# Two-layer graph network on one core: the prologue in blocks of four, its weights on two queues beside the table, the sums zeroed block by block

## The chip, the cores and the metric

The kernel runs on one core of a Trainium2 chip. The metric is the device time of one execution in microseconds (us); lower is better. The timed figure is the median of three runs. Beside it stands one more execution that the hardware profiler recorded; every duration of a single instruction below is from that one.

## The reference, cut to what matters

A graph has 6250 nodes with 160 features (64 scalars and 32 three-vectors) and 200000 edges, sorted by their destination. Two message-passing layers run one after the other. Each one mixes the node features linearly, makes a weight vector per edge from the edge's attributes, multiplies the features of the edge's source node by it, and adds the products up over the edges of each destination node.

```python
# layer 0, per node and per edge (layer 1 has the same shape)
x1 = (xs * attr_a) @ Ws_l1_a + (xs * attr_c) @ Ws_l1_c   # and the same for the vectors
weight = silu(edge_attr_10 @ W_fc1) @ W_fc2
edge_feat = weight * x1[edge_src] * edge_attr            # several products
agg = segment_sum(edge_feat, edge_dst, num_segments=n)
out = C_S * self_part + C_X * ((agg @ W_l2_a) + (agg @ W_l2_c)) @ W_l3
# then residual and layer norm; layer 1 follows on the result
```

## The kernel before, in words

**Edges in tiles, tiles in groups.** The edges come in NT = 1563 tiles of 128. Consecutive tiles form 284 groups of 3 to 12 tiles; because the edges are sorted, all edges of a group fall into a window of W = 32 destination nodes. The sums of all nodes stay in SBUF for a whole layer, in two tiles `sm` (128 x 4 x 6304) and `sr` (128 x 6304) (lines 115 and 116).

**The loop.** `windows(i, loads, work)` (from line 465) is run for layer i = 0 and then i = 1. It goes through 391 units of four tiles. Per unit GpSimd (POOL) issues four indirect DMAs, which gather the source nodes' rows of a table in DRAM (line 583); TensorE (PE) makes the hidden layer (`pa`) and the edge weights (`pw`), VectorE (DVE) builds the selection matrices (`sel`, line 617) and the products (`mid`, lines 599 and 604), TensorE adds the products up in PSUM (`pg`), turns the result (`pt`), and VectorE adds it to `sm` and `sr` at a row that it reads from `base` (lines 667 and 669). Gathers run four units ahead of the sums: there are eight gather buffers of two tiles. Node blocks whose sums are complete are finished in between (`second_nodes`, `last_nodes`). At line 404 and 405 `second_nodes` clears the block's sums with VectorE for layer 1.

**The prologue.** All that stands ahead of the loop is straight-line code:

* SP loads the nodes in 7 chunks of 7 blocks (line 124); ACT's queue loads `nv`, the first layer's weights `wl1` by way of `spread` (lines 138 to 155), 15 short runs of `base` (line 171) and the destinations `raw` (line 175).
* From `base` and `raw` it makes `off`, each edge's row within its window (lines 183 to 196), and writes it to DRAM as `rel`; the loop reads it back in pieces, `dr` (line 500). From `off` it works out a flag (lines 199 to 216): whether every edge lies within its window. If not, a general and slow path runs in place of `windows`.
* `first_nodes` (lines 251 to 266) makes the gather table of layer 0. For each of the 49 node blocks it transposes the features with TensorE (two transposes, `turned`, lines 219 to 228), copies both out with ACT, multiplies them by `wl1` (two products: 128 x 256 and 32 x 64, `mixed`, line 230), and combines the two halves with ACT and VectorE. One DMA on SP's queue per chunk writes the rows.
* The weights of the loop are put together in `fc1`, `fc2`, `wsc`, `wh`, `wo`, `rm0`, `rr0`, `rm1`, `rr1` (lines 273 to 351), by DMAs on SP's queue. `rm0` and `rr0` are filled by ten DMAs from SBUF to SBUF out of four products of TensorE (lines 314 to 329).
* GpSimd zeroes `sm` and `sr` whole, in two instructions (line 354).
* The pools of the prologue are given back at line 355 (`prologue.close()`); the loop's `loads` and `edges` pools take that memory.

**What sets the order.** The framework orders the instructions of each engine by a simulation of its own, as far as data allow. In the loop, TensorE's instructions are kept in program order (`pinned`, lines 238 to 248); in the prologue they are not. [...]

## Time and profile before

| | |
|---|---|
| median of three timed runs | 6722.72 us (6715.26 to 6724.2) |
| the profiled execution's own time | 4272.91 us |
| its span | 4271.1 us |
| mean granted TensorE clock in it | 0.908 |
| TensorE busy | 3661.5 us (86% of the span) |
| GpSimd busy | 3021.2 us (71%) |
| VectorE busy | 2957.8 us (69%) |
| first gather starts | 153.58 us |

The profiled execution is 2450 us shorter than the timed median. Busy times count matmuls whose ends are modelled. A line of the groups says: line of the kernel, engine, operation, output<-inputs, shapes, count, then busy time and mean ns of one, then the idle time of that engine just before and what ended most of it.

### The profile page before, as it was taken

How to read it: one execution, taken by the hardware profiler on the slowest of the kernel's cores; microseconds unless marked ns; L12 is line 12 of the kernel's file. 1: busy time of each engine (PE TensorE's matmuls, PEld its weight loads, DVE VectorE, ACT ScalarE, POOL GpSimd, SP SyncE). 2: the span in 40 equal slices, each digit the busy share in tenths (PEclk: the TensorE clock that was granted, in tenths of full speed). 3: DMA queues.
4: the chain of work that ended last, by engine and by line, in shares of the span. 5: the costliest groups of instructions: out<-in, count | busy, mean ns of one | idle time of the engine just before them, and what ended most of it. 6: DMA issues, size and time to landing. Idle time of an engine off the chain costs nothing.

```text
span 4271.1 us, 137680 instructions
## 1 busy us (share of the span) xinstructions
PE 3661.5 (86%) x53873; PEld 2656.1 (62%) x53873; DVE 2957.8 (69%) x10736; ACT 1065.0 (25%) x2506; POOL 3021.2 (71%) x3192
## 2 busy tenths in 40 slices
PE   7787879888999999999988888888888888888887
PEld 4555556566666666666655666666666666666665
DVE  5466666666667677766655777777777777777887
ACT  2211111222222233333221001121222222333443
POOL 2477777777777777766635777777777777777775
PEclk9989999899999999999986988888898898898888
DMA  2233333333333333332212333333443344434443
GB/s 82 67 74 74 77 76 77 80 79 82 79 84 83 83 85 85 81 76 75 71 48 76 93 100 99 99 99 99 102 103 102 97 110 104 106 101 108 107 108 76
DMA packets 312505, 374.13 MB, mean 88 GB/s; under 512 B 98379, under 2 KB 256783, under 8 KB 311851
## 3 DMA queue, kind: packets, MB, share of 16 engines
q0 software_dynamic: 150016, 256.20, 24.4%
q1 hardware_dynamic: 132406, 91.31, 8.0%
q10 hardware_dynamic: 29429, 17.75, 1.4%
q8 instruction: 430, 7.05, 0.7%
q14 instruction: 224, 1.84, 0.1%
HBM read 343.19 MB, written 21.60 MB: 85 GB/s over the span
## 4 chain that ended last, share of the span: by engine, by line
PE 40%; issue 17%; DMA 14%; POOL 13%; DVE 10%; ACT 2%; DVEq 1%; SPq 0%; POOLq 0%; ACTq 0%
POOL g L583 13%; DMA g<-table,src 13%; PE pw L241 12%; PE pg L241 9%; PE pa L241 8%; PE pn L241 7%; DVE mid L604 3%; PE pt L246 2%; DVE sel L617 2%; DVE mid L599 2%; DMA e<-in_e 1%; PE pn L246 1%; DVE sm L667 1%; ACT L363 1%; DVEq L664 1%
## 5 line engine op out<-in xcount | busy, mean ns | idle before, releaser
L583 POOL DMA_INDIRECT g<-table,src x3126 | 2990.1, 957 | 1218.5 <-issue 720.4
L241 PE MATMUL pw<-fc,h 100*128 100x192 f32 (+1 forms) x6252 | 1279.6, 375 | 197.2 <-DVE mid L604 171.3
L241 PEld LDWEIGHTS pg<-mid,sel 128*32 128x32 f32 x40638 | 953.2, 118 | 489.0 <-issue 485.9
L241 PEld LDWEIGHTS pw<-fc,h 100*128 100x128 f32 (+1 forms) x6252 | 955.1, 201 | 352.7 <-issue 162.8
L604 DVE TENSOR_TENSOR mid<-g,pw 128x192 f32<-128x192 f32 x3910 | 1170.2, 346 | 0.0
L599 DVE TENSOR_TENSOR mid<-pw,g 128x256 f32<-128x256 f32 x1564 | 660.8, 423 | 720.2 <-DMA g<-table,src 406.0
L241 PE MATMUL pg<-mid,sel 128*32 128x64 f32 (+4 forms) x40638 | 1130.6, 255 | 0.0
L617 DVE SCALAR_TENSOR_TENSOR sel<-iota,dr,ea 128x128 f32<-128x128 f32 x3126 | 951.4, 346 | 240.4 <-PE pg L241 227.6
L241 PE MATMUL pa<-e,fc 128*100 128x512 f32 (+1 forms) x1566 | 748.8, 563 | 123.1 <-DMA e<-in_e 122.8
L542 ACT ACTIVATE h<-pa 100x512 f32<-100x512 f32 x391 | 233.5, 597 | 1203.0 <-PE pa L241 1176.4
L241 PEld LDWEIGHTS pa<-e,fc 128*100 128x100 f32 (+1 forms) x1566 | 265.5, 193 | 250.9 <-issue 125.3
L554 ACT ACTIVATE h<-pa 128x256 f32<-128x256 f32 x392 | 150.4, 384 | 1022.8 <-PE pa L241 1003.7
L246 PE MATMUL pt<-ident,r 128*96 128x128 f32 (+1 forms) x852 | 229.0, 292 | 15.6 <-DVE sr L669 13.8
L646 ACT ACTIVATE r<-pg 128x96 f32<-128x96 f32 (+1 forms) x568 | 154.9, 274 | 315.4 <-PE pg L241 209.8
L667 DVE TENSOR_TENSOR sm<-pt,sm 96x128 f32 (+1 forms) x568 | 162.7, 286 | 89.6 <-PE pt L246 81.8
L246 PEld LDWEIGHTS pt<-ident,r 128*96 128x96 f32 (+1 forms) x852 | 106.0, 124 | 133.7 <-issue 67.3
L241 PE MATMUL pn<-rm,sm 96*128 96x128 f32 (+4 forms) x980 | 160.4, 318 | 17.2 <-DVE sm L667 14.2
L241 PEld LDWEIGHTS pn<-rm,sm 96*128 96x128 f32 (+3 forms) x980 | 154.3, 218 | 25.2 <-DVE sm L667 18.4
L554 ACT ACT_TABLE_LOAD x94 | 120.6, 1283 | 122.7 <-PE pa L241 99.4
L241 PE MATMUL pn<-rr,sr 64*128 64x128 f32 (+2 forms) x196 | 62.1, 403 | 80.2 <-DVE sr L669 79.2
L241 PE MATMUL pt<-ident,r 128*32 128x32 f32 x2272 | 85.9, 203 | 47.9 <-DVE sr L669 46.2
L241 PEld LDWEIGHTS pt<-ident,r 128*32 128x32 f32 x2272 | 89.5, 118 | 53.7 <-issue 47.5
(118 smaller groups left out, 1508.6 us busy)
## 6 DMA issues: line engine op xcount, KB each, us to landing
g<-table,src POOLq DMA_INDIRECT x3126
e<-in_e SPq DMA_DIRECT2D x781, 64.0 KB
e<-in_e SPq DMA_DIRECT2D x390, 20.0 KB
ea<-in_ea_main SPq DMA_DIRECT2D x64, 96.0 KB
xself<-no ACTq DMA_DIRECT2D x48, 96.0 KB
no<-xself SPq DMA_DIRECT2D x48, 96.0 KB
nx<-in_x_main SPq DMA_DIRECT2D x48, 80.0 KB
xmid<-nx ACTq DMA_DIRECT2D x48, 80.0 KB
```

What stands on the lines that cost most here:

```text
L241: r = nc.tensor.matmul(*args, **kw)
L246: r = nc.tensor.transpose(*args)
L363: nc.scalar.activation(mv[:n, 1:2], mv[:n, 1:2], AF.Sqrt, bias=eps[:n])
L542: nc.scalar.activation(h[:100, :n], p[:100, :n], AF.Silu)
L554: nc.scalar.activation(h[:kk, c0:c1], p[:kk, c0:c1], AF.Silu, scale=0.125)
L583: nc.gpsimd.indirect_dma_start(out=g[:n, j, :], out_offset=None, in_=table[i][:, :], in_offset=bass.IndirectOffsetOnAxis(ap=of(t)[0], axis=0))
L599: nc.vector.tensor_tensor(two, q[:n, :m, 0:2 * S].rearrange("p j (k d) -> p j k d", k=2), gs, OP.mult)
L604: nc.vector.tensor_tensor(o[:, :, at:at + 96].rearrange("p j (c d) -> p j c d", c=3), gv, q[:n, :m, None, w0:w0 + V].to_broadcast([n, m, 3 ...
L617: made["last"] = nc.vector.scalar_tensor_tensor(s[:n, j], iota[:n, None, :].to_broadcast([n, 4, W]), w, e[:, :, None].to_broadcast([n, 4, ...
L646: nc.scalar.activation(r[:, :w], pg[:, :w], AF.Copy)
L664: b = nc.vector.value_load(base[0:1, g:g + 1], min_val=0, max_val=NP - W)
L667: nc.vector.tensor_tensor(sm[:h, :, at], pt[:h, :P].rearrange("p (c w) -> p c w", c=4), sm[:h, :, at], OP.add)
```

## The change

The number of blocks per chunk, `BG`, goes from 7 to 4, and `ZERO = 8` is new. `pinned` is true from the start, so the prologue's TensorE instructions keep the written order, too. The rest, part by part:

```diff
-BG = 7
+BG = 4
+ZERO = 8
+def zeroed(g):
+    b = ZERO + 4 + (GROUPS[g][0] + GROUPS[g][1] - 1) // 4
+    return NP if b >= NB else b * P
...
-    rel = dram.tile([P, NT], F32, name="rel")
...
+    def zero(b):
+        c = slice(b * P, b * P + P if b < NB - 1 else NP)
+        nc.vector.memset(sm[:, :, c], 0.0)
+        nc.vector.memset(sr[:, c], 0.0)
+    pinned = [True]
...
+    first = (const.tile([P, CH, 1], I32, name="src0"), const.tile([P, CH, 4], F32, name="ea0"))
+    nc.sync.dma_start(first[0], a["src_main"][:, :CH, :])
+    nc.sync.dma_start(first[1], a["ea_main"][:, :CH, :])
...
+    spread(l1[:, 0], "Ws_l1_a", "Wv_l1_a", S, nc.scalar)
+    spread(l1[:, 1], "Ws_l1_c", "Wv_l1_c", S, nc.scalar)
     ident = const.tile([P, P], F32, name="ident")
     make_identity(nc, ident)
+    for j, (k, q) in enumerate((("a", nc.scalar), ("c", nc.gpsimd))):
+        for r in range(0, P, V):
+            q.dma_start(l1z[r:r + V, j, :], a[f"Wv_l1_{k}"])
+    nc.gpsimd.dma_start(nv[:, :NB - 1, :], a["nv_main"])
+    nc.gpsimd.dma_start(nv[:tail_n, NB - 1, :], a["nv_tail"])
...
-        while g1 < NG and GROUPS[g1][1] == GROUPS[g0][1] and (g1 + 1 - g0) * GROUPS[g0][1] <= 180:
+        while g1 < NG and GROUPS[g1][1] == GROUPS[g0][1]:
...
-        nc.scalar.dma_start(base[:, g0:g1], bass.AP(tensor=d.tensor, offset=d.offset + t0 * P,
+        nc.gpsimd.dma_start(base[:, g0:g1], bass.AP(tensor=d.tensor, offset=d.offset + t0 * P,
...
-    nc.scalar.dma_start(raw[:, :NT - 1], a["dst_main"][:, :, 0])
-    nc.scalar.dma_start(raw[:tail_e, NT - 1:], a["dst_tail"])
+    nc.gpsimd.dma_start(raw[:, :NT - 1], a["dst_main"][:, :, 0])
+    nc.gpsimd.dma_start(raw[:tail_e, NT - 1:], a["dst_tail"])
...
+    nc.gpsimd.dma_start(fc1[0][:10], a["W_fc1"])
...
+        nc.gpsimd.dma_start(fc2[0][:, at:at + n], a["W_fc2"][:, c0:c0 + n])
...
+        nc.gpsimd.dma_start(w23[:, at:at + n], a[k])
...
+    def turn_nodes(bs, x):
+        m, n = len(bs), rows_of(bs[0])
+        p = psum.tile([P, 512], F32, name="pw", bufs=3)
+        for j in range(m):
+            transpose(p[:, j * P:j * P + n], x[:n, j, 0:P], ident[:n, :n])
+        last = work.tile([P, BG * V], F32, name="xz")
+        nc.vector.tensor_copy(last[:n, :m * V].rearrange("p (j d) -> p j d", d=V), x[:n, 0:m, P:D])
+        z = psum.tile([P, 512], F32, name="pa", bufs=1)
+        transpose(z[:m * V, :n], last[:n, :m * V], ident[:n, :n])
+        xt = work.tile([P, BG * P], F32, name="xt", bufs=2)
+        zt = work.tile([P, P], F32, name="zt", bufs=2)
+        w = (m - 1) * P + n
+        nc.vector.tensor_copy(xt[:, :w], p[:, :w])
+        nc.scalar.activation(zt[:m * V, :n], z[:m * V, :n], AF.Copy)
+        return xt, zt
+    def send_nodes(bs, xt, zt):
...
+        for j, b in enumerate(bs):
+            tag, k = (("pg", 2), ("pn", 1), ("pg", 2), ("pt", 1))[j]
...
+            matmul(q[:, :, 0:P], xt[:, j * P:j * P + n], l1, start=True, stop=True)
+            matmul(q[:, :, P:D], zt[v, :n], l1z[v], start=True, stop=True,
+                   tile_position=(j * V, 0))
+            t = rows[:n, j, :]
+            nc.scalar.activation(t, q[:, 0, :], AF.Copy, scale=nv[:n, b, 0:1])
+            nc.vector.scalar_tensor_tensor(t, q[:, 1, :], nv[:n, b, 1:2], t,
+                                           op0=OP.mult, op1=OP.add)
...
-    off = pre.tile([P, NT], F32, name="off")
+    off = const.tile([P, NT], F32, name="off")
...
+    def check():
...
+        p = psum.tile([P, 512], F32, name="pa", bufs=1)
+        matmul(p[:, :NG], ones, basef, start=True, stop=True)
+        for g0, g1 in segments:
...
+            nc.vector.tensor_tensor(o, o, p[:, g0:g1, None].to_broadcast([P, m, n]), OP.subtract)
...
+        nc.vector.tensor_reduce(ends[:, 0:1], off, AX.X, OP.max)
+        nc.vector.tensor_reduce(ends[:, 1:2], off, AX.X, OP.min)
...
+        transpose(p[:1, :P], over, ident)
...
+    for c, (bs, x) in enumerate(zip(chunks, xs)):
+        now = bs, turn_nodes(bs, x)
+        if previous:
+            send_nodes(previous[0], *previous[1])
+        previous = now
+        if c == 8:
+            check()
+    send_nodes(previous[0], *previous[1])
...
+    for b in range(ZERO):
+        zero(b)
...
-    for t in (sm, sr):
-        nc.gpsimd.memset(t, 0.0)
     prologue.close()
...
+            if c == 0:
+                s, e = first
...
-            nc.sync.dma_start(w[:, :t1 - t0], rel[:, t0:t1])
...
+            return s[:n, k, :], off[:n, t:t + 1], e[:n, k, :]
...
+            if i == 0 and ZERO + 4 + u < NB:
+                zero(ZERO + 4 + u)
```

In words, for the parts that are cut: the flag also asks that a group's window lies in rows that are zeroed by then (`zeroed`). The second layer's weights `wh` and `wo` become one tile `who`, loaded like `wsc` on SP's queue. `rm0` and `rr0` are filled by six copies of VectorE out of PSUM, from eight small products of TensorE, in place of four products and ten DMAs. `rm1` and `rr1` are still loaded by 16 DMAs of SP, and scaled by seven VectorE instructions in place of 16. In the written order the weights of `wsc`, `who`, `fc1[1]`, `fc2[1]`, `rm1` and `rr1` (40 DMAs on SP's queue) stand behind the table's last store. GpSimd's queue issues 29 direct DMAs: 4 of `l1z`, 2 of `nv`, 11 of `base`, 2 of `raw`, 1 of `fc1`, 3 of `fc2`, 6 of `w23`. The loop is otherwise as it was.

## Prediction

> **What bounds the kernel now.** I read the page first. Its largest row is the gather on GpSimd:

> ```profile
> L583 POOL DMA_INDIRECT g<-table,src x3126 | 2990.1, 957 | 1218.5 <-issue 720.4
> ```

> A gather takes 957 ns, and about 300 ns pass to the next one: 3126 x 1.257 = 3929 us of a span of 4271.1. In the profiled execution the loop thus follows GpSimd, and what stands ahead of the first gather is paid in full. It starts at 153.58 us; the change is almost all in that stretch. So next the stretch by stages (columns: window, its length, then busy us of PE, its weight loads, DVE, ACT, POOL; granted clock, DMA share, GB/s):

> ```profile
> 0.00:33.00 33.00, 2.52 (x11) 1.90 (x11) 29.54 (x14) 2.03 (x5) 31.14 (x66) 1.00 0.53 159
> 33.00:60.00 27.00, 26.96 (x88) 17.88 (x87) 12.38 (x37) 6.42 (x27) 0.00 (x0) 1.00 0.17 56
> 60.00:119.80 59.80, 59.80 (x167) 36.39 (x166) 14.20 (x50) 19.60 (x84) 0.00 (x0) 1.00 0.15 43
> 119.80:145.00 25.20, 24.11 (x71) 14.94 (x70) 5.05 (x16) 7.75 (x32) 0.00 (x0) 1.00 0.14 45
> 145.00:154.30 9.30, 0.04 (x1) 0.07 (x1) 2.14 (x6) 0.00 (x0) 0.72 (x1) 1.00 0.19 41
> ```

> Three parts: 33 us with TensorE nearly idle, 111 us in which it is busy throughout, and a tail of 9 us in which it is idle again. The instructions in order of time (start, us, instruction) say why the first part is empty:

> ```profile
> 4.31 27.48 DVE L298 TENSOR_SCALAR own<-nv 128x96 f32<-128x96 f32 x1 [2.45 <-DMA nv<-in_nv_main]
> ...
> 5.33 21.11 POOL L354 MEMSET sm<- 128x25216 f32 x1
> ...
> 26.39 5.34 POOL L354 MEMSET sr<- 128x6304 f32 x1
> ...
> 32.95 1.22 PE L241 MATMUL pt<-wl,xt 128*128 128x256 f32 x2
> ```

> A small VectorE instruction issued at 4.31 ends at 31.79; GpSimd's memsets end at 31.73. VectorE stood still while GpSimd zeroed, and everything waited behind it. In the second part the work on two node blocks repeats every 4.28 us:

> ```profile
> 124.09 1.11 PE L246 MATMUL pw<-ident,xg 128*128 128x128 f32 x4
> ...
> 125.00 1.06 PE L241 MATMUL pt<-wl,xt 128*128 128x256 f32 x2
> ...
> 125.99 0.69 PE L241 MATMUL pt<-wl1z,xt 32*128 32x64 f32 x2
> ...
> 126.60 1.22 PE L241 MATMUL pn<-wl,xt 128*128 128x256 f32 x2
> ...
> 128.37 1.11 PE L246 MATMUL pw<-ident,xg 128*128 128x128 f32 x4
> ```

> From start to start: four transposes 0.91 us (0.23 each), the wide product 0.99, the narrow one 0.61. The third part, from the chain that ended last (start, us, what):

> ```profile
> 144.46 0.30 SPq L266
> ...
> 148.74 1.85 DMA rm<-w23s
> ...
> 152.03 1.56 DMA e<-in_e
> 153.59 1.10 POOL g L583
> ```

> The table's last store goes out at 144.46; then SP issues the last seven of the ten copies into `rm0` and `rr0`, and only when the last has landed (150.59) is the prologue's memory free for the loop's loads.

> **How this stands to the median.** Span 4271.1 plus 1.8 outside is the profiled 4272.9. The median is 6722.7; no view shows the other 2450. There is one hint. The 512-column product `pa`, between 160 and 168 us and then between 190 and 210 us:

> ```profile
> L241 PE MATMUL pa<-e,fc 128*100 128x512 f32 x4 | 3.8, 1059 | 0.0
> L241 PE MATMUL pa<-e,fc 128*100 128x512 f32 x8 | 4.1, 592 | 0.0
> ```

> TensorE runs at about half rate up to 168 us, although the granted clock is printed as 1.00 there. If timed runs stayed at that rate, TensorE would bind: its 3661 us busy times 1.63 (192-column products, 540 to 332 ns) to 1.79 (`pa`) is 5970 to 6550, an estimate, not far below 6723. In that reading, or if gathers are slower there, the prologue is as in the profile (TensorE is at half rate in it already), so I carry the microseconds over unscaled.

> **The change, part by part.**

> *Zeroing.* Off GpSimd go 26.4 us of memset. On VectorE, block by block: the existing clear of one block takes 485 + 165 ns (lines 404, 405), so 8 blocks in the prologue cost 5.2 us beside 100 us of TensorE work, and 42 in the loop 0.65 us per unit of 5.0 us, in which VectorE is about 64% busy: hidden, up to 27 us if VectorE were the bound. [...] GpSimd waited for line 405 five times in 49, 1.5 us in all. I take 0 and keep 2 (scaled from 1.5) to 27.

> *Start.* What now precedes the first product: `ident` (ready at 1.4), the first chunk of x (320 KB instead of 560 KB, whose first came at 4.96; about 4), `l1` by ACT's queue (six issues at 0.45 to 0.59, landing near 6.5), and `l1z` half by ACT, half by GpSimd. A direct DMA of GpSimd's is in no row; nearest is the gather, 1.25 from start to start. Four `l1z` then are issued by 6.5 and land, at some 2.5 as for gathers, at 9.0; `nv` follows at 11.5, and only ACT's evacuation needs it, with four PSUM banks to fill meanwhile. I take 9.0 for the first wide product, 33 before. Bounds: 6.5 if a direct one costs SP's 0.45, 20 if 4. All 29 take 36 us plus some 8 of memsets: done near 44, while `base` and `raw` are needed near 75. [...]

> *TensorE per chunk of four.* Five transposes, not eight: 5 x 0.23 + 4 x (0.99 + 0.61) = 7.5, with before's gap (0.17 per pair) 7.7, where two pairs were 8.56. Twelve chunks 92.4, the tail block 2.1; less two chunks' transposes done ahead of 9.0 (2.3): 92.2. VectorE per chunk: 0.2 + about 0.6 + 4 x 0.383 = 2.3; ACT 0.25 + 4 x 0.394 = 1.8: both hidden. The fifth transpose waits for VectorE's gathering copy; queued behind the fourth combination of the chunk before, it comes 0.4 to 0.5 late. I take 0.25 x 12 = 3, bounds 0 to 6.

> *The check.* It was spread among the products; now TensorE is pinned, and the transpose of `over` stands ahead of chunk 9's transposes. It waits for VectorE: cast of `off` 0.95, eleven subtractions (0.95 ns for each of 1563 elements, 0.17 for each instruction, from 343 ns for 180) 3.4, two reductions of 1.77 and some 0.4 of small ones; with the products' last combinations ahead, about 9, of which TensorE covers under 1. Behind it are all of TensorE's later products, so ACT, VectorE and the stores wait, too. I take 8, bounds 4 (casts hoisted) to 11.

> *Tail.* After the last product: ACT 0.39, VectorE 0.37, store 0.30, landing about 2: 3.1. `src` and `ea` lie in SBUF by then, so the gather starts at 9.0 + 92.2 + 3 + 8 + 3.1 = 115.3. Saved: 153.6 - 115.3 = 38. TensorE itself, if it is the bound: eight small products of some 0.5 end at 116.2, then clearing and loading `e` (as before, 3.7 from release to product, less 1.3 for loads that are gone) gives about 119 against 154.3: 35. The 40 weight issues on SP (0.45 to 0.6, 18 to 24 us) I take as fitted in between stores, as the framework did with 20 of them around 27 to 33 and 54 to 60; written order would put `e` up to 20 later, of which some 13 is covered by 16 gathers ahead (16 x 1.25 = 20, less the 6.6 us in which the first products come).

> Dropping `rel`, `dr` (66 loads) costs and gains nothing: `sel` waits for PSUM and gathers, not for `dr`, beyond the start.

> Sum: span 4271 - 38 = 4233; median 6722.7 - 38 = 6685.

> **The rivals.**

> *TensorE wakes in the prologue* (10%). Its work is denser, and at 168 us full rate came after dense products. 92 us would become some 50: saved about 80, median 6643. Against: the view by stages has 60 us of unbroken busy time at half rate.

> *Late stages* (10%): check at 11, start at 20, or SP's queue in written order. Saved 14 to 30; 6700.

> *Nothing to be seen* (4%): two of these together, within 0.2% (13.4 us, about what this measurement can tell from no change); 6717.

> *Slower* (5%): GpSimd's direct DMAs. The first gather stands behind all 29 of them. Beyond (153.6 - 8) / 29 = 5.0 us each it comes later than today; at 6.0 it starts at 182, 28 later: 6751. Against: 0.95 us for a gather of 128 rows, and only `base` moves more pieces (284 in 11 DMAs).

> **How the numbers follow.** Likeliest (71%): saved 30 to 50, 6673 to 6693; 6685. The range 6640 to 6706 takes in nearly all of it, most of the first rival and half of the late cases. Faster 0.91, same 0.04, slower 0.05.

> **What would show it.** First wide product near 9 us; 7.7 us per chunk; a gap of about 8 us on TensorE beside two reductions of 1.77; gather near 115; gathers still 1.25 apart in units 1 to 42. Wrong if TensorE's 512-column product is at 0.6 us before the loop, if GpSimd's direct DMAs take over 2 us, or if the timed runs' 2450 us move with the prologue.

## The result and the profile after

The changed kernel takes 6680.15 us (median of 18 runs, 6632.67 to 6721.85), the kernel before 6712.29 beside it (18 runs, 6682.11 to 6799.66). The ratio is 0.9946, 95% interval 0.992 to 0.9972: of 6712 us some 36 are saved, 19 to 54. Forecast were 38, and 6685 us in the range 6640 to 6706. The profiled execution of the changed kernel has a span of 6658.2 us and took 6660.39.

The first gather starts at 96.74 us, against 153.58 in the profile before: 57 us earlier, and more than the time shows. The stretch ahead of it by stages (columns: window, its length, then busy us of PE, its weight loads, DVE, ACT, POOL; granted clock, DMA share, GB/s):

```profile
0.00:9.49 9.49, 2.50 (x10) 1.99 (x11) 7.51 (x28) 1.56 (x2) 8.48 (x22) 1.00 0.71 218
9.49:49.07 39.58, 39.58 (x166) 24.66 (x165) 21.10 (x62) 14.73 (x40) 12.52 (x85) 1.00 0.49 149
49.07:56.42 7.35, 0.00 (x0) 0.03 (x1) 6.97 (x21) 0.11 (x1) 0.00 (x0) 0.74 0.22 55
56.42:88.50 32.08, 32.08 (x83) 19.64 (x84) 9.57 (x28) 7.39 (x20) 0.00 (x0) 0.50 0.10 32
88.50:96.74 8.24, 3.26 (x20) 2.23 (x18) 4.84 (x14) 0.39 (x1) 0.00 (x1) 0.50 0.16 49
```

The start is 9.5 us where it was 33. In the second and fourth rows TensorE has no idle time, but the second holds twice as many products in a quarter more time. The clock in the table can't be read up to the first change of rate (it is printed as 1.00 before that); the products' durations can. The same wide product of TensorE in the same execution, at 45.71 and at 59.26 us (two passes each):

```profile
45.71 0.70 PE L134 MATMUL pn<-l,xt 128*128 128x256 f32 x2
...
59.26 1.22 PE L134 MATMUL pn<-l,xt 128*128 128x256 f32 x2
```

From 18.5 to 52.6 us TensorE ran at full rate, and then at half rate again. In the profile before it was at half rate until 168 us. A chunk of four blocks takes 8.03 us at half rate and 4.46 at full. That is a difference between two executions, not between the kernels, as the unchanged kernels show below. To compare stages, I therefore state the first gather as it would be at half rate throughout: each microsecond of the table at full rate adds 8.03 / 4.46 - 1 = 0.80. Here these are 30.6 us (18.5 to the gap at 49.1), so 96.7 + 24.5 = 121.2. The change is then worth 153.6 - 121.2 = 32 us ahead of the first gather.

The gap in the third row, in order of time (start, us, instruction; in brackets the idle time before it and what ended that):

```profile
49.52 2.42 DVE L290 TENSOR_TENSOR off<-off,pa 128x444 f32<-128x444 f32 x11
...
52.56 1.77 DVE L294 TENSOR_REDUCE ends<-off 128x1 f32<-128x1563 f32 x1
54.25 1.77 DVE L295 TENSOR_REDUCE ends<-off 128x1 f32<-128x1563 f32 x1
```

```profile
56.42 0.37 PE L139 MATMUL pa<-ident,over 128*1 128x128 f32 x1 [7.36 <-DVE over L299]
```

TensorE stands 7.36 us, as its pinned order has the transpose of `over` ahead of the next chunk. And the tail, where SP's store at 92.77 is late:

```profile
89.08 0.61 PE L134 MATMUL pg<-l1z,zt 32*106 32x64 f32 x2
...
91.81 0.28 DVE L363 COPY rm<-pw 64x128 f32<-64x128 f32 x1 [2.92 <-PE pw L134]
92.10 0.22 DVE L364 COPY rm<-pw 32x64 f32<-32x64 f32 x1
92.36 0.38 DVE L265 SCALAR_TENSOR_TENSOR rg<-pg,nv,rg 106x160 f32<-106x160 f32 x1
...
92.77 0.29 SPq L272 DMA_DIRECT2D table<-rg  x1
```

The last block's combination (L265) stands on VectorE behind two copies into `rm0`, and those wait for `w23`'s eight products.

### The profile page after: what moved, and what is told of

It reads as the page before. It is cut to its first block, busy times and chain, and to the rows that moved or that the text cites. A ratio compares the mean times of both kernels' runs of the same rounds, so it can differ in the third digit from the quotient of the medians.

```text
span 6658.2 us, 137406 instructions
## 1 busy us (share of the span) xinstructions
PE 4903.6 (74%) x53817; PEld 3300.5 (50%) x53817; DVE 2948.5 (44%) x10849; ACT 1055.2 (16%) x2421; POOL 3029.3 (45%) x3232
## 3 DMA queue, kind: packets, MB, share of 16 engines
q8 instruction: 430, 7.05, 0.4%
## 4 chain that ended last, share of the span: by engine, by line
PE 69%; issue 19%; another core or an unknown queue 5%; DVE 4%; ACT 1%; DVEq 1%; DMA 0%; ACTq 0%; SPq 0%
PE pg L134 23%; PE pw L134 22%; PE pa L134 12%; PE pn L134 6%; PE pt L139 3%; PE pt L134 2%; DVE sel L681 1%; DVE mid L668 1%; PE pn L139 1%; DVE mid L663 1%; DVEq L728 0%; DVE sm L731 0%; ACT L618 0%; ACT L426 0%
## 5 line engine op out<-in xcount | busy, mean ns | idle before, releaser
L134 PE MATMUL pg<-mid,sel 128*32 128x64 f32 (+4 forms) x40638 | 1737.7, 278 | 784.3 <-issue 773.6
L134 PEld LDWEIGHTS pg<-mid,sel 128*32 128x32 f32 x40638 | 1241.6, 130 | 1728.4 <-issue 1707.3
L134 PE MATMUL pw<-fc,h 100*128 100x192 f32 (+1 forms) x6252 | 1575.5, 456 | 188.8 <-issue 139.0
L681 DVE SCALAR_TENSOR_TENSOR sel<-iota,off,ea 128x128 f32<-128x128 f32 x3126 | 958.6, 345 | 1553.4 <-remote 496.3
L134 PEld LDWEIGHTS pw<-fc,h 100*128 100x128 f32 (+1 forms) x6252 | 1143.9, 247 | 407.2 <-issue 302.7
L134 PE MATMUL pa<-e,fc 128*100 128x512 f32 (+1 forms) x1566 | 927.4, 681 | 25.9 <-issue 17.4
L134 PEld LDWEIGHTS pa<-e,fc 128*100 128x100 f32 (+1 forms) x1566 | 329.3, 236 | 213.9 <-issue 203.8
L134 PE MATMUL pt<-ident,r 128*32 128x32 f32 x2272 | 159.4, 218 | 234.1 <-issue 181.2
L134 PE MATMUL pn<-rm,sm 96*128 96x128 f32 (+4 forms) x980 | 223.9, 395 | 94.6 <-DVE sm L731 72.6
L134 PEld LDWEIGHTS pn<-rm,sm 96*128 96x128 f32 (+3 forms) x980 | 211.1, 284 | 108.0 <-DVE sm L731 76.2
L618 ACT ACT_TABLE_LOAD x94 | 120.6, 1283 | 187.3 <-PE pa L134 115.6
```

The source lines that it names most:

```text
L134: r = nc.tensor.matmul(*args, **kw)
L618: nc.scalar.activation(h[:kk, c0:c1], p[:kk, c0:c1], AF.Silu, scale=0.125)
L681: made["last"] = nc.vector.scalar_tensor_tensor(s[:n, j], iota[:n, None, :].to_broadcast([n, 4, W]), w, e[:, :, None].to_broadcast([n, 4, ...
```

## The experiments

**My theory** is the prediction's: 24 us at the start, which it put down to GpSimd's memset, the rest from fewer TensorE instructions and a shorter tail, less the check's gap. **The rivals**: that the profile's 57 us are the gain of the change (a denser prologue wakes TensorE), or that little is gained in the prologue and the time comes from the loop. All runs in a table; "before" is the time of the kernel before on the same chip. "At full" is how long TensorE was at full rate, up to the check's gap or to its last product ahead of the loop, and the last column is the first gather at half rate throughout, worked out as above.

| run | before, us | ratio, 95% | first gather, us | at full, us | at half rate, us |
|---|---|---|---|---|---|
| b0: before, unchanged (one execution) | 6551 | – | 126.97 | 33.7 | 153.9 |
| a0: changed, unchanged | 6551 | 0.9947 (0.9921 to 0.9973) | 117.70 | 3.7 | 120.6 |
| a1: the same, another chip | 4264 | 0.9913 (0.988 to 0.9946) | 114.35 | 8.2 | 120.9 |
| e_zero_only | 6551 | 0.9984 (0.9958 to 1.001) | 114.67 | 38.5 | 145.5 |
| e_loads | 4260 | 0.9945 (0.9925 to 0.9966) | 121.87 | 9.8 | 129.7 |
| e_pool_zero | 4260 | 0.9985 (0.9964 to 1.0005) | 132.06 | 9.8 | 139.9 |
| e_check | 6551 | 0.9918 (0.9876 to 0.996) | 113.61 | 0 | 113.6 |
| e_tail | 4260 | 0.9904 (0.9873 to 0.9935) | 113.27 | 0 | 113.3 |
| e_warm | 4260 | 0.9858 (0.9809 to 0.9907) | 83.54 | to 53.7 | – |
| e_spread | 4264 | 0.9891 (0.9851 to 0.993) | 115.06 | 0 | 115.1 |
| e_best | 4264 | 0.9851 (0.9825 to 0.9878) | 85.39 | to 54.9 | – |
| e_best2 | 4263 | 0.9838 (0.9802 to 0.9875) | 70.52 | all | – |

### Both kernels, unchanged

> The kernel before, unchanged: one more look. The changed kernel's record has a span of 6658 us and the first record of the kernel before 4271, so the two loops can't be compared. Theory A (what is saved ahead of the first gather is paid out one for one): this record shows a span near 6710, the first gather again near 153.6 us, and from there to the end as long as in the changed kernel (about 6561 us) within 30. Theory B (the loop gives part of it back): its loop is shorter than the changed kernel's by 20 to 40 us.

> The changed kernel, unchanged: does TensorE come to full rate in the prologue each time? Theory A (its work sets the rate): full rate from about 18 us to the gap before the transpose of over, half rate from there to the loop, first gather at 96 to 98 us. Theory B (chance of the execution): half rate throughout, and the first gather at 120 to 125 us. Time 0.992 to 0.997 of before under both.

> The changed kernel as it is, on the chip of these runs. If the saving is the 32 us of the prologue and nothing else, it is the same in microseconds wherever the rest of the kernel runs at another speed: 30 to 40 us under before, a ratio of 0.991 to 0.993 where before takes 4260 us. If it scales with the span, 0.9946 in every place. First gather 95 to 122 us, by when TensorE comes to full rate.

In this second profile the kernel before came to full rate too, at 83.2 us, and its first gather was at 127, not 153.6. The wide product that takes 1.22 us in the prediction's lines takes 0.70 here:

```profile
109.62 0.70 PE L241 MATMUL pn<-wl,xt 128*128 128x256 f32 x2
```

The changed kernel came to full rate at 18.5, 66.4 and 58.5 us in three executions, so a0 bears out neither of its two theories as they stand. Stated at half rate, before gives 153.6 and 153.9, after 121.2, 120.6 and 120.9. So the change moves the first gather by 33 us; the rest is when TensorE happens to wake. The rival that the 57 us are the change's falls.

On the two chips with 4260 and 4264 in the table the kernel before takes 4.26 ms, on the chip of a0 and in the result 6.5 to 6.7 ms. The saving is 36 us of 6712, 35 of 6551 and 37 of 4264 (from the ratios; the intervals reach some 14 to 18 us to either side): the same microseconds rather than the same share, as far as the intervals tell. That speaks for the prologue and against the loop. So does the profile: in a1, from the first to the last gather 4077.6 us pass, in the profile of before 4085.8. What b0 was to decide, whether the loop gives something back, it can't: on its chip these times are 6332.3 (a0), 6335.6 (e_zero_only), 6353.6 (e_check) and 6357.8 us (b0), and a0 and e_check, which have the same loop, differ by 21 us, a0 and b0 by 26. One kernel on two chips, a0 and then a1, the gather's row (busy us, mean ns | idle us before it, and what ended most of it):

```profile
L647 POOL DMA_INDIRECT g<-table,src x3126 | 3025.9, 968 | 3399.1 <-DVE mid L668 2140.9
```

```profile
L647 POOL DMA_INDIRECT g<-table,src x3126 | 2987.7, 956 | 1179.5 <-issue 714.9
```

A gather costs the same, and GpSimd is idle 2220 us longer, most of it for VectorE (`mid`), which takes TensorE's products. In a0 TensorE's products start 600 to 900 ns apart 1448 times (111 times in a1), and it is at half rate for 2939 us (829 in a1). Why those gaps come on one chip and not on the other, no run tells.

### e_zero_only: before, with VectorE's zeroing alone

```diff
-    for t in (sm, sr):
-        nc.gpsimd.memset(t, 0.0)
+    for b in range(ZERO):
+        zero(b)
...
+            if i == 0 and ZERO + 4 + u < NB:
+                zero(ZERO + 4 + u)
```

Its flag does not ask for the zeroed rows.

> The kernel before with one part of the change: the sums zeroed block by block by VectorE, eight blocks ahead of the loop and one in each of its first 42 units, instead of two memsets of GpSimd. Theory A (GpSimd's memsets held VectorE up): VectorE's small instructions on nv no longer end at 31.8 us, the first wide product moves from 33 to 14 to 22 us (then the waits for ACT's queue and base end last), and the first gather from 153.6 to 135 to 143. Theory B (the start is bound by the loads in any case): the first gather moves by under 5 us. Zeros in the loop: no longer gathers under A and B[...].

Too hopeful. The first wide product came at 24.5 us, the first gather stated at half rate at 145.5: 8 us gained (by the ratio 10 us, with an interval that takes in zero). VectorE no longer stood still; ScalarE's queue was next. ScalarE, and the DMAs on its queue, in order of time:

```profile
7.83 11.54 ACTq L177 DMA_DIRECT2D base<-in_dst  x15
...
22.89 1.28 ACT L232 ACT_TABLE_LOAD   x1 [22.89 <-DVE basef L189]
24.18 0.28 ACT L232 ACTIVATE xt<-pw 128x128 f32<-128x128 f32 x1
```

Fifteen issues of `base` take ScalarE 11.5 us, and the first copy of transposes comes only behind them. TensorE's first product with `basef` waits for the same loads, until 22.62. VectorE's standstill had covered this.

### e_loads: the same, with nv, base and raw on GpSimd's queue

```diff
-    nc.scalar.dma_start(nv[:, :NB - 1, :], a["nv_main"])
+    nc.gpsimd.dma_start(nv[:, :NB - 1, :], a["nv_main"])
...
-        nc.scalar.dma_start(base[:, g0:g1], bass.AP(tensor=d.tensor, offset=d.offset + t0 * P,
+        nc.gpsimd.dma_start(base[:, g0:g1], bass.AP(tensor=d.tensor, offset=d.offset + t0 * P,
```

`raw` and the tail of `nv` likewise; its flag does not ask for the zeroed rows either.

> The kernel before with the sums zeroed by VectorE (its first wide product was at 24.5 us, against 33.0 before), and nv, the bases and the destinations loaded through GpSimd's queue instead of ScalarE's. Theory A (behind VectorE's standstill ScalarE's own issues were next late: twelve microseconds of them stood ahead of its copies of the first transposes): the first wide product comes at 9 to 13 us and the first gather about 12 us earlier than in the version without it (near 133 at half rate throughout, 114.7 plus 0.8 us for each us at full rate there). Theory B [...]: first wide product at 20 to 25 us, nothing gained.

Theory A held: first wide product at 8.61 us, ahead of GpSimd's issues for the destinations (13.10 and 13.80 us), and first gather 16 us earlier (129.7). These two edits alone bring 24 of the change's 33 us (by the ratio 23, 14 to 32). The other 9 us no run isolates: the chunks of four and the tail bring them, less the check's gap, which e_check takes alone.

### e_pool_zero: the changed kernel, zeroed by GpSimd again

```diff
-    for b in range(ZERO):
-        zero(b)
+    for t in (sm, sr):
+        nc.gpsimd.memset(t, 0.0)
...
-            if i == 0 and ZERO + 4 + u < NB:
-                zero(ZERO + 4 + u)
```

> The changed kernel with one part undone: the sums are zeroed by GpSimd's two whole memsets again, where VectorE's first eight blocks stood, and the blocks of the first loop are not zeroed one by one. Theory A (what held VectorE in the kernel before, GpSimd's memset, holds it wherever it runs): the first product with the weights is on time at about 9.5 us, but somewhere in the first 50 us a VectorE copy stands for about 27 us, the table ends about 25 us later than in the changed kernel (first gather near 146 us where TensorE is at half rate throughout, instead of 121), and the time is about 25 us above the changed kernel's: a ratio to before near 0.998. Theory B (in the changed kernel GpSimd's memsets come behind its 29 transfers [...] while TensorE has a chunk in reserve): about 5 us of the hold show, the ratio stays near 0.995. In both the loop is up to 3 us shorter, because VectorE's forty-odd zeroings of a block in it are gone.

Theory A, but for the size. GpSimd reaches the memsets at 25.2 us, behind its transfers, and in that instant VectorE stops. GpSimd, VectorE and TensorE in order of time:

```profile
25.22 21.10 POOL L327 MEMSET sm<- 128x25216 f32 x1
46.27 5.34 POOL L327 MEMSET sr<- 128x6304 f32 x1
```

```profile
25.78 25.91 DVE L242 COPY xz<-xg 128x128 f32<-128x128 f32 x1
25.92 25.92 DVE L282 CAST basef<-base 1x284 f32<-1x284 int32 x1
51.76 0.36 DVE L265 SCALAR_TENSOR_TENSOR rg<-pg,nv,rg 128x160 f32<-128x160 f32 x1
```

```profile
52.17 1.22 PE L134 MATMUL pg<-l,xt 128*128 128x256 f32 x2 [18.80 <-DVE rg L265]
```

A copy that takes 0.2 us elsewhere ends at 51.69, just behind GpSimd's last memset (51.61). TensorE has 7.6 us of work in hand and then stands for 18.8; the first gather, stated at half rate, comes 19 us later than in the changed kernel. In time 6 us are left of what the change saves (-2 to 15). The cast behind the copy took 25.92 us and ended at 51.84; in the profile before it was the `tensor_scalar` on `own` that took 27.48 us. What the two engines contend for, no run shows. Taken alone, the new zeroing brought 8 us; taken out of the whole, it costs 19. The edits don't add up, since each stall stands in the shadow of the other.

### e_check: the check split

```diff
-        p = psum.tile([P, 512], F32, name="pa", bufs=1)
+        p = psum.tile([P, 512], F32, name="pw", bufs=3)
         matmul(p[:, :NG], ones, basef, start=True, stop=True)
...
+    def flags():
...
+        p = psum.tile([P, 512], F32, name="pw", bufs=3)
+        transpose(p[:1, :P], held["over"], ident)
...
     send_nodes(previous[0], *previous[1])
+    flags()
```

`flags` holds what of the check stood from the first reduction of `limits` on.

> The changed kernel with the check in two parts: its product goes to another PSUM tag and the transpose of over stands behind the last block's products, so nothing on TensorE waits for VectorE. Theory A (the wait of 7.4 us is what puts TensorE back to half rate): no gap, four chunks and the tail at 4.5 instead of 8.0 us, the first gather 20 to 23 us earlier than in the changed kernel, near 75. Theory B (TensorE falls back to half rate in any case): only the gap goes, the first gather 6 to 8 us earlier, near 89. In time 0.3% or 0.1% less than the changed kernel.

The gap is gone, and the first gather at half rate is 7 us earlier. My expectation that TensorE would then stay awake fell: it never woke, though from 8.65 us on it had no idle time but for 0.08 us. Its transposes, chunk by chunk, 8.03 us apart:

```profile
40.17 1.11 PE L139 MATMUL pw<-ident,xg 128*128 128x128 f32 x4
...
48.20 1.11 PE L139 MATMUL pw<-ident,xg 128*128 128x128 f32 x4
...
56.22 1.11 PE L139 MATMUL pw<-ident,xg 128*128 128x128 f32 x4
```

### e_warm: e_check, and six products of 512 columns at the start

```diff
+    warm = pre.tile([P, 512], F32, name="warm")
+    nc.vector.memset(warm, 0.0)
+    p = psum.tile([P, 512], F32, name="pt", bufs=1)
+    for _ in range(6):
+        matmul(p, warm[:, :P], warm, start=True, stop=True)
```

> The version with the check split, with six products of 128x512 on a tile of zeros put ahead of the first transposes, on TensorE alone (work added, nothing taken away). In the version without them TensorE stayed at half rate through the whole prologue: chunks of 8.03 us, first gather at 113.6. Theory A (the rate comes up after a stretch in which TensorE has no idle time at all, and the start, with its waits for tiles, is what denies it that): the granted clock is at 1.0 within 20 us of the start, chunks of four take 4.46 us, first gather near 72 us if the burst costs 5 us, the time some 40 us under that version's. Theory B (the rate in the prologue is by chance of the execution): the burst costs 5 to 10 us at the start, chunks are at 8.03 us or come to 4.46 anywhere, first gather between 85 and 122.

Full rate came at 5.94 us, 4.5 us into the products, and the chunks took 4.46 us; the first wide product came 1.3 us later than in e_check (10.32). But full rate lasted only to 53.7. TensorE, then VectorE:

```profile
1.48 7.62 PE L134 MATMUL pt<-warm 128*128 128x512 f32 x12 [1.48 <-DVE warm L165]
...
50.85 0.60 PE L134 MATMUL pg<-l,xt 128*128 128x256 f32 x2
...
53.64 1.17 PE L134 MATMUL pn<-l,xt 128*128 128x256 f32 x2 [1.83 <-DVE rg L271]
```

```profile
49.78 1.77 DVE L300 TENSOR_REDUCE ends<-off 128x1 f32<-128x1563 f32 x1
51.47 1.77 DVE L301 TENSOR_REDUCE ends<-off 128x1 f32<-128x1563 f32 x1
```

A wait of 1.83 us for VectorE, busy with the check's two reductions, and from then on half rate to the end of the table. At full rate TensorE no longer covers the check.

### e_tail: e_check, with w23's products and copies ahead of the last block

```diff
+    p = psum.tile([P, 512], F32, name="pw", bufs=3)
+    q = p[:96, :192].rearrange("p (j d) -> p j d", j=2)
+    for j in range(2):
...
     send_nodes(previous[0], *previous[1])
     flags()
```

> The version with the check split, with the eight products of w23 and the copies into rm0 and rr0 moved ahead of the last block's products. Theory A (the tail of 7 us is 3 us of VectorE's wrong order: the last block's combination stands behind the copies into rm0, which wait for w23's products): from the last wide product to the first gather 4 to 5.5 us instead of 8.2, but TensorE's eight products, 2 us, are now on the path; first gather 111 to 113 at half rate throughout, against 113.6. Theory B (the tail is the store's landing and nothing else moves): the distance stays 8 us and the gather comes 2 us later, near 115.6.

From the last wide product to the first gather 6.05 us pass instead of 8.39, but 2.1 us of small products are now ahead of it: 113.3 instead of 113.6, no gain to speak of. From the store's issue to the gather it is 4.0 us in both; the forecast had 2.3.

### e_spread, e_best and e_best2: towards a better version

e_spread is e_check with the check in pieces over five chunks, and with w23's products in the last block's PSUM bank, so that its combination goes first (the pieces of the check are left out here):

```diff
-            tag, k = (("pg", 2), ("pn", 1), ("pg", 2), ("pt", 1))[j]
+            tag, k = (("pg", 2), ("pn", 1), ("pg", 2), ("pt", 1))[j] if n == P else ("pn", 1)
...
-    p = psum.tile([P, 512], F32, name="pw", bufs=3)
+    p = psum.tile([P, 512], F32, name="pn", bufs=1)
     q = p[:96, :192].rearrange("p (j d) -> p j d", j=2)
```

e_best is e_spread with e_warm's six products.

> The same without the six products at the start. Theory A (the burst is what brings the rate up): half rate through all or most of the prologue, first gather 108 to 112 (113.6 less the 3 us of the tail), or down to 90 where the rate comes up by itself late; ratio to before 0.990 where before takes 4260 us. Theory B (only gaps hold the rate down, and the start's gaps end at 9 us): full rate from about 20 us on, first gather near 75, as with the burst.

> Six products on a tile of zeros at the start, the check spread over five chunks (no VectorE stretch long enough to stop TensorE), its transpose behind the last block, and w23's products in the last block's PSUM bank, so that its combination comes before the copies into rm0. Theory A (the rate rises after a stretch without idle time and falls again after a gap of about 2 us or more): full rate from about 6 us to the end of the table, chunks of 4.46 us throughout, last wide product near 63 us, first gather at 68 to 70; the time about 80 us below the kernel before, 45 below the changed kernel: ratio to before 0.981 where before takes 4260 us, 0.988 where it takes 6600. Theory B (the fall at 53.7 us in the run before was by chance, as the rises in other runs): full rate from about 6 us again but falling at some other point, first gather 72 to 90, ratio 0.983 to 0.988 where before takes 4260.

```diff
+        if c + 2 < len(chunks):
+            ahead.append(lasts(chunks[c + 2], xs[c + 2]))
...
+        if 7 <= c <= 10:
+            k = c - 7
+            nc.vector.tensor_reduce(ends[:, k:k + 1], off[:, half:] if k % 2 else off[:, :half],
+                                    AX.X, OP.max if k < 2 else OP.min)
```

`lasts` is the copy of `xz`, made two chunks ahead; the reductions are cut into halves.

> The last version with its remaining gaps of TensorE taken out: VectorE's copies for the gathered transposes are made two chunks ahead, and the check's two reductions of 1.77 us each are cut into halves over four chunks. Theory A (a gap of about 2 us is what ended full rate at 53.7 and 54.9 us in the two runs with the products at the start; without such a gap it lasts): full rate from about 7 us to the end of the table, last wide product at 64 to 67 us, first gather at 70 to 74, ratio to before 0.980 to 0.983 where before takes 4260 us. Theory B (full rate ends after a fixed 47.8 us, the same in both, gap or no gap): it ends at about 54 us again though TensorE has no gap there, first gather 82 to 86, ratio 0.985.

Theory A: full rate from 7.15 us to the last product ahead of the loop, which ends at 67.45, the whole table. Its profile by stretches, past the start (columns as above):

```profile
20.00:34.00 14.00, 14.00 (x68) 8.71 (x67) 10.43 (x24) 5.62 (x16) 5.99 (x71) 1.00 0.34 91
34.00:47.00 13.00, 13.00 (x63) 8.07 (x62) 8.86 (x28) 5.16 (x15) 0.00 (x0) 1.00 0.33 92
47.00:60.00 13.00, 13.00 (x63) 8.28 (x61) 8.95 (x20) 5.37 (x15) 0.00 (x0) 1.00 0.29 82
```

No idle time, and some 63 products in 13 us throughout. The first gather is at 70.5. It is the fastest version tried: 4183.22 us against 4262.58 before, and 4230.47 for the changed kernel on the same chip. By the ratio it saves 69 us of before's time (53 to 84), where the change saves 37 (23 to 51). The timed runs of the three versions with the products at the start lie within 6, 9 and 7 us of one another (4 to 6 runs each), those of a1 within 28 (6 runs) and of e_spread within 24 (4). That fits a scatter which comes in good part from the moment at which TensorE wakes.

## Why the prediction was right, and where it was not

- **Start, 33 to 9.0**: right, 9.5. The memset's hold on VectorE was shown by e_zero_only and e_pool_zero. But it was two stalls, one behind the other: the memset's hold on VectorE, and ScalarE's own issues. The prediction moved the second one without naming it.
- **GpSimd's direct DMAs at 1.25 us each**, and the slower rival that decides at 5.0: mis-sized. They took 0.50 to 0.69 us (ScalarE's 0.32 to 0.59). The 29 were issued by 21.3 us, not 36 to 44. This didn't show, as nothing waited for it.
- **Chunk of four, 7.7 us**: 8.03 at half rate, 4 us more over twelve. The sum took 0.99 us for a wide product, the first of a pair, and one gap of 0.17; in e_check, as in the rows of e_warm at half rate, it is 1.16 to the next product in three of four blocks. **Wait for the gathering copy, 3 us**: 0; VectorE made it ahead of need. These two cancel.
- **The check, 8 us, bounds 4 to 11**: right, 7.36. At half rate e_check brought 7 us for it.
- **Tail, 3.1 us**: 7.05 from the end of the last block's products. Two terms: VectorE's order put the `rm0` copies first (the combination could run at 90.1 and ran at 92.4: +2.2), and the store took 4.0 us to the gather where 2.3 were put down (+1.7). Moving those copies buys little: 0.3 us in e_tail, where the eight products come ahead of the last block instead, and some 1.3 of the tail in e_spread, where three small instructions of the check stand ahead of the combination.
- **Zeroing in the loop, 0 (0 to 27)**: right. On one chip it took from first to last gather 4083.7 and 4082.3 us in e_tail and e_warm with the zeroings, and 4085.1 in e_pool_zero without. (The prediction's least cost of 2 us isn't 1.5 scaled from 49 blocks to 42; that is 1.3.) e_loads, on the same chip with the loop of before, took 4086.9: dropping `rel` and `dr`, put at nothing, may be worth 3 to 5 us, which single traces can't show.
- **SP's forty issues fitted between the stores**: right, done by 56.3 us.
- **Sum**: 115.3 was forecast for the first gather, 120.9 is the mean of three at half rate. Start 0.5, chunks 4, copy wait -3, check -0.6 and tail 4 make 4.9 of the 5.6 us. So the saving ahead of the first gather was 33 us, not 38. That the timed 36 came so near to 38 is in part luck, as its interval is 19 to 54.
- **Half rate throughout the prologue**: the step that failed. It stays so in four of the fourteen executions with a profile (e_check, e_tail, e_spread, and the first profile of before), and b0 shows full rate in the kernel before as well. "TensorE wakes in the prologue" was put as a rival for the changed kernel alone, worth 80 us; by one of its own signs of being wrong, full rate ahead of the loop, the prediction failed here. In both kernels it is an accident of the execution, worth 0 and 27 us in two profiles of the kernel before, and 24.5, 2.9 and 6.6 in three of the changed one. That it leaves the difference is likely from the timed 36 us, but these profiles are too few to show it.
- **Microseconds carried over unscaled**: supported by the three pairs at 4264, 6551 and 6712 us (a fixed share would save 23 of 4264, which is just the end of a1's interval). The 2450 us between profile and median ahead of the change are most likely the same two levels, and they did not move with the prologue. The hint behind it was only half right: where the kernel takes 6.5 ms TensorE is at full rate for about as long (3488 us in a0, 3342 in a1), and what is added, 2110 of 2265 us, is time at half rate.

What stays open: why on some chips TensorE's products come 0.6 to 0.9 us apart so often, and at what moment the table's work brings full rate up by itself.

## What to carry to other kernels

Behind the stall that a profile names, look for what would have been late anyway on the other queues: here the memset's hold of 27 us hid 12 us of ScalarE's own DMA issues, and removing the hold alone gave 8 of the 24 us that both gave. Before you compare two profiles stage by stage, read the rate of TensorE off one product's duration in each (the wide one took 0.70 or 1.22 us here), and state both at one rate. If a stage is bound by TensorE at half rate, a few dense products ahead of it can bring up the rate (here six of 512 columns did, 4.5 or 5.7 us after their start, in three runs of three). In both runs here that then had a wait of about 2 us for VectorE it was gone again, so cut long VectorE instructions there into pieces.

## What the runs showed of the hardware

- **The same work runs at either rate.** The table ran at half rate for 97 us in e_check, with 0.08 us of idle time, and at full rate for 54 us in e_best2. Six dense products brought full rate 4.5 or 5.7 us after their start (three runs of three); in the eleven executions without them it came at 18.5 us or later, in four not ahead of the loop at all. After gaps of 1.83, 2.23 and 7.36 us it was gone, after one of 0.78 not. The length of the gap isn't all: in e_loads the last of the small products ahead of the loop ended at 111.65 us, and the mean clock from 112 to 122 us was 0.51, so full rate was gone within 0.7 us of it. What sets the moment of a change, no run shows.
- **A copy of 0.2 us was held for 25.9 us** by a GpSimd memset, in the middle of the work (e_pool_zero), though no data go from one to the other.
- **One kernel, two levels**: 4.23 ms in a1 and 6.49 in a0 for the same instructions, with gathers of 956 and 968 ns.
